# A five-stage convolution kernel on one Trainium2 core: the rows of its DRAM staging buffer take 4608 bytes instead of 4096

## The chip, the core and the metric

The kernel runs on one core of a Trainium2 chip. The metric is the device time of one execution in microseconds (us). Before the change the median of three runs is 16687.61 us.

## The reference, cut to what matters

```python
# x: (4, 512, 512, 16)
def _L0_conv_ref(x, h0, numerators, denumerator):      # the convolution by FFT
    H_full = h0 + H_cc                                 # (16, 16, 1024, 513), from two 8x8 polynomials
    X = jnp.fft.rfft2(x, s=(2 * l1, 2 * l2), axes=(-3, -2))
    Y = jnp.einsum('...hwi,ijhw->...hwj', X, H_full)   # 16x16 channel mix at each frequency
    y = jnp.fft.irfft2(Y, s=(2 * l1, 2 * l2), axes=(-3, -2))
    return y[..., :l1, :l2, :]

x = x + _L0_conv_ref(_gn(x), h0, numerators, denumerator)   # group norm, convolution, add
x = x + _L1_conv_ref(_gn(x), kernel, bias, radius)          # a 3x3 layer, not touched here
```

The change lies in the middle of the first line: the convolution of all rows of the half-transformed image with the half-transformed filter.

## The kernel before, in words

The kernel is written with the Tile framework, which puts in the semaphore waits. It has five stages, one after the other: the filter (`filter_phase`), the transform of the image along one axis (`forward_phase`), the convolution along the other axis (`conv_phase`), and the inverse transform and the 3x3 layer (both in `last_phase`). The stages hand their results over in DRAM: `g_d` holds the filter, `x_d` the image, `y_d` the result of the convolution. Rows of these buffers carry a padding of `PITCH` = 1024 elements already.

`conv_phase` takes the stretch from about 4.7 ms to 13.7 ms. It works through 513 rows `n`, one frequency of the first axis each (row 0 is done as two). For each row it transforms the image row, multiplies it with the filter at 128 frequencies `f`, and transforms back. The image row must be there in eight copies that are shifted against each other by 16 partitions (`C` = 16), so that one matmul per frequency does the work of a short convolution. The parts of one row are:

- `load_x` (L748) brings the image row into `x`, `x_part` (L777) multiplies it on TensorE with the row's own transform matrix into `px`, and the result is copied into part 0 of `xe`, a tile of 128 partitions with eight parts of 1024 fp32 (4096 bytes) each.
- `x_late` stores part 0 to the DRAM buffer `xf_d[n % 4]`, makes the rotated other half `xl` with six operations on GpSimd (L798, L799, L800), and stores that too. Both stores go out from GpSimd's queue at L791. Each writes 112 rows of 4096 bytes. `half_shift` (L809) makes part 4 of `xe` on ScalarE without DRAM.
- `load_xe` (L815) reads the other six parts back, as two DMAs of 1.5 MB from SP's queue. DMA `t` (1 and 5) gives partition p, part t + i, the row p + 16 (t + i) of `xf_d`, for i from 0 to 2. Each is therefore 384 pieces of 4096 bytes, and most rows are read several times.
- `load_g` (L736) brings the filter row, 1 MB, and `g_part` (L829) transforms it into `gh`.
- `mix` (L845) multiplies `gh` with `xe`; `over_q` (L866 to L884) and `over_g` (L903, L914) transform back and store to `y_d` from GpSimd's queue.

`step(n)` fixes the order. It starts with `load_x(n + 3)`, `load_g(n + 2)` and `load_xe(n + 1)`. Then come four quarters; each holds a quarter of `mix(n)`, of `g_part(n + 1)` and of `over_q(n - 1)`, and the first quarter also `x_part(n + 2)` and `x_late(n + 2)`. So the stores of a row are issued one step ahead of its loads, and its loads one step ahead of its `mix`. In the trace SP issues in the order first `xe` load, `g`, second `xe` load, `x`, and the first of them waits for the landing of the second store.

`XF` is the length of a row of `xf_d` in elements: 128 x 2 x 4 = 1024, which is 4096 bytes. A buffer is `[16 * C, XF]`, 256 rows without a gap.

Of the kernel before, what the change touches and what calls it, by code (L numbers as in the profile page):

```python
# [40 lines left out]
F32 = mybir.dt.float32  # L41
# [5 lines left out]
P = 128  # L47
N = 512
B = 4
C = 16  # L50
# [4 lines left out]
Y_ROW = 2 * B * S * C * 8  # L55
PITCH = 1024
XF = F * 2 * B
GN_EPS = 1e-5
L1_EPS = 1e-12

# [143 lines left out]
def bc(ap, axis, shape):  # L204
    return ap.unsqueeze(axis).to_broadcast(shape)
# [328 lines left out]
def group_stats(nc, pool, psum, mean_m, eps_t, mv):  # L534

    mu = pool.tile([P, 8], F32, name="gn_mu")
    nc.vector.tensor_copy(mu, mv[:, :, 0])
    pm = psum.tile([P, 8], F32, name="gn_ps", tag="gn_ps")
    nc.tensor.matmul(pm, mean_m, mu, start=True, stop=True)
    mean = pool.tile([P, 8], F32, name="gn_mean")  # L540
    nc.vector.tensor_copy(mean, pm)
    d = pool.tile([P, 8], F32, name="gn_d")
    nc.vector.tensor_sub(d, mu, mean)
    nc.vector.tensor_mul(d, d, d)
    nc.vector.tensor_add(d, d, mv[:, :, 1])
    pv = psum.tile([P, 8], F32, name="gn_ps2", tag="gn_ps")
    nc.tensor.matmul(pv, mean_m, d, start=True, stop=True)
    sd = pool.tile([P, 8], F32, name="gn_sd")
    nc.scalar.activation(sd, pv, AF.Sqrt, bias=eps_t)
    scale = pool.tile([P, 8], F32, name="gn_scale")  # L550
    nc.vector.reciprocal(scale, sd)
    bias = pool.tile([P, 8], F32, name="gn_bias")
    nc.vector.scalar_tensor_tensor(bias, mean, -1.0, scale, ALU.mult, ALU.mult)
    return scale, bias
# [36 lines left out]
def joined(nc, pool, a, b):  # L591

    mv = pool.tile([P, 8, 2], F32, name="mv")
    d = pool.tile([P, 8], F32, name="mv_d")
    nc.vector.tensor_add(mv, a, b)
    nc.vector.tensor_scalar(mv, mv, 0.5, None, ALU.mult)
    nc.vector.tensor_sub(d, a[:, :, 0], mv[:, :, 0])
    nc.vector.tensor_mul(d, d, d)
    nc.vector.tensor_add(mv[:, :, 1], mv[:, :, 1], d)
    return mv  # L600


def forward_phase(tc, cst, x, mvs, x_d):
    nc = tc.nc
    with ExitStack() as ctx:
# [13 lines left out]
        eps_t = cp.tile([P, 1], F32, name="x_eps")  # L619
        nc.gpsimd.memset(eps_t, GN_EPS)  # L620
        norm = [group_stats(nc, sm, ps_s, mean_m, eps_t, joined(nc, sm, mvs[2 * b], mvs[2 * b + 1]))
# [74 lines left out]
def conv_phase(tc, cst, g_d, x_d, y_d):  # L696
    nc = tc.nc
    with ExitStack() as ctx:
# [14 lines left out]
        ig = load_const(nc, cp, cst, "ig").rearrange("p (s c n) -> p s c n", s=4, c=2)  # L713
        late = load_const(nc, cp, cst, "late").rearrange("p (v f) -> p v f", v=3)

        xf_d = [tc.dram_tile([16 * C, XF], F32, name=f"xf_d{n}") for n in range(4)]


        rows = [(0, 0, 0), (0, 0, 1)] + [(n // P, n % P, None) for n in range(1, N)]
# [64 lines left out]
        def x_late(n):  # L784

            xe = state["xe", n][:, 0]
            fl = xe.rearrange("p f h c k -> p f (h c k)")

            def store(half, t):
                at = slice(C, P) if half == 0 else slice(0, P - C)  # L790
                nc.gpsimd.dma_start(out=xf_d[n % 4][half * P :, :][at], in_=t[at].rearrange("p f x -> p (f x)"))  # L791

            store(0, fl)
            xl = xlp.tile([P, F, 2, 2, 2], F32, name="xl")
            u = xlp.tile([P, F, 2, 2, 2], F32, name="xu")
            for c in range(2):
                for h in range(2):
                    nc.gpsimd.tensor_mul(u[:, :, h, c], xe[:, :, h, 1 - c], bc(late[:, 1 + c], 2, [P, F, 2]))  # L798
            nc.gpsimd.tensor_mul(xl.rearrange("p f h c k -> p f (h c k)"), fl, bc(late[:, 0], 2, [P, F, 8]))  # L799
            nc.gpsimd.tensor_add(xl.rearrange("p f h c k -> p (f h c k)"),  # L800
                                 xl.rearrange("p f h c k -> p (f h c k)"),
                                 u.rearrange("p f h c k -> p (f h c k)"))
            store(1, xl.rearrange("p f h c k -> p f (h c k)"))
            state["xl"] = xl
# [7 lines left out]
        def load_xe(n):  # L812
            src = xf_d[n % 4]
            for t in (1, 5):
                nc.sync.dma_start(  # L815
                    out=state["xe", n][:, t : t + 3].rearrange("p t f h c k -> p t (f h c k)"),
                    in_=bass.AP(tensor=src.tensor, offset=src.offset + t * C * XF,
                                ap=[[XF, P], [C * XF, 3], [1, XF]]),
                )

        def g_part(n, j):
# [100 lines left out]
        def step(n):  # L922
# [9 lines left out]
            if row(1):  # L932
                load_xe(n + 1)
# [29 lines left out]
def last_phase(tc, cst, x, y_d, yw_d, t_d, kern, bias, radius, out):  # L963
    nc = tc.nc
    with ExitStack() as ctx:
# [11 lines left out]
        eps_t = cp.tile([P, 1], F32, name="l_eps")  # L977
        nc.gpsimd.memset(eps_t, GN_EPS)
        eps1 = cp.tile([P, 1], F32, name="l_eps1")
# [409 lines left out]
def body(tc, ins, cst, out):  # L1389
    g_d = [tc.dram_tile([P, G_ROW + PITCH], F32, name=f"g_d{r}") for r in range(4)]  # L1390
    x_d = [tc.dram_tile([P, X_ROW + PITCH], F32, name=f"x_d{r}") for r in range(4)]
    y_d = [tc.dram_tile([P, Y_ROW + PITCH], F32, name=f"y_d{r}") for r in range(4)]
    yw_d = [tc.dram_tile([C, N, N], F32, name=f"yw_d{b}") for b in range(B)]
    t_d = [[tc.dram_tile([N, P, C], F32, name=f"t_d{b}_{w}") for w in range(4)] for b in range(B)]
    with tc.tile_pool(name="s_mv", bufs=2 * B) as mp:
        mvs = []
        with tc.tile_pool(name="s_in", bufs=1) as xp:
            beside = image_stats(tc, xp, mp, ins["x"], mvs)
            filter_phase(tc, cst, ins["L0_conv_h0"], ins["L0_conv_numerators"][0],
                         ins["L0_conv_denumerator"], g_d, beside)  # L1400
            for _ in beside:
                pass
        forward_phase(tc, cst, ins["x"], mvs, x_d)
    conv_phase(tc, cst, g_d, x_d, y_d)
    last_phase(tc, cst, ins["x"], y_d, yw_d, t_d, ins["L1_conv_kernel"], ins["L1_conv_bias"],
               ins["L1_conv_radius"], out)
# [30 lines left out]
```

## Time and profile before

| what | value |
|---|---|
| median of three runs | 16687.61 us (16677.77 to 16700.49) |
| the profiled execution's own time | 16676.9 us |
| its span, first to last instruction | 16675.0 us |
| granted TensorE clock, mean | 0.970 |
| TensorE busy in the span | 15084.4 us, 90% |
| DMA traffic | 4543.40 MB, mean 272 GB/s |
| `xe` loads from `xf_d` | 1026, 1536.0 KB each |
| stores into `xf_d` | 2 x 513, 448.0 KB each |

The engines are TensorE (PE for its matmuls, PEld for its weight loads), VectorE (DVE), ScalarE (ACT), GpSimd (POOL) and SyncE (SP, which only issues DMAs). The profile comes from one execution. A line such as "PE pm L845 <- DMA xe<-xf_d" says that TensorE sat idle ahead of an instruction of line 845, which writes `pm`, until that DMA had landed; "issue" stands for idle time with no cause in the profile. Beside the instructions the trace has a record of each DMA packet, with its queue, start, length of time and size; q1 is the queue of SP and q0 that of GpSimd.

### The profile page before, as it was taken

The numbers are of one execution on the slowest core, as the hardware profiler recorded it, in microseconds if no ns is written. First come the engines' busy times: TensorE is split into PE (matmuls) and PEld (weight loads), VectorE is DVE, ScalarE is ACT, GpSimd is POOL, SyncE is SP. The second block draws the span as 40 slices with busy tenths as digits, with TensorE's granted clock in tenths as the row PEclk, the third lists the DMA queues.
The fourth block names the chain that finished last, engine by engine and source line by source line (L and its number), as shares of the span: only waits on it lengthen the run. The fifth ranks groups of instructions, "written<-read, shape, count | busy, mean of one in ns | idle before, by whom it ended". The sixth has DMA issues, their size and how long they took to land. (4 is left out here: it accounts for less than half of the span.)

```text
span 16675.0 us, 545650 instructions
## 1 busy us (share of the span) xinstructions
PE 15084.4 (90%) x232588; PEld 11256.3 (68%) x232588; DVE 10610.7 (64%) x22299; ACT 9049.8 (54%) x18799; POOL 10372.0 (62%) x10669
## 2 busy tenths in 40 slices
PE   7999999998988898888888898888888888988888
PEld 5555555554557777777777777777777777867777
DVE  8999999993545555555555555555555552357877
ACT  5666666663345555555555555555555551027888
POOL 7777777772346666666666666666666660237766
PEclk7999999999999999999999999999999999989999
DMA  4888788878878888888888888888888886885531
GB/s 134 231 237 236 233 241 234 237 227 259 248 267 323 325 326 317 321 320 318 321 324 324 325 325 321 324 324 321 324 321 321 324 322 230 312 291 164 169 108 70
DMA packets 2914698, 4543.40 MB, mean 272 GB/s; under 512 B 126114, under 2 KB 2094460, under 8 KB 2801422
## 3 DMA queue, kind: packets, MB, share of 16 engines
q1 hardware_dynamic: 2703070, 3836.37, 67.4%
q0 software_dynamic: 172336, 605.00, 9.4%
q10 hardware_dynamic: 36864, 67.13, 1.2%
q8 instruction: 1833, 30.03, 0.7%
q14 instruction: 595, 4.87, 0.1%
HBM read 3030.71 MB, written 1477.31 MB: 270 GB/s over the span
## 5 line engine op out<-in xcount | busy, mean ns | idle before, releaser
L829 PE MATMUL pg<-c_dg,g 64*128 64x128 f32 x32832 | 2837.4, 290 | 357.0 <-ACT gh L729 186.6
L845 PE MATMUL pm<-xe,gh 128*32 128x64 f32 x131328 | 2386.6, 222 | 538.5 <-issue 286.2
L845 PEld LDWEIGHTS pm<-xe,gh 128*32 128x32 f32 x131328 | 2007.6, 110 | 1133.5 <-issue 933.1
L829 PEld LDWEIGHTS pg<-c_dg,g 64*128 64x128 f32 x32832 | 2286.2, 190 | 692.3 <-issue 260.3
L874 DVE TENSOR_TENSOR z<-zq,pz 128x256 f32<-128x256 f32 x2052 | 861.6, 420 | 2667.5 <-ACT zq L873 2597.6
L727 DVE COPY gh<-pg 128x512 f32<-128x512 f32 x2046 | 1409.9, 689 | 1242.8 <-PE pg L829 1237.6
L449 PE MATMUL pt<-ev_in,c_todd 128*128 128x512 f32 x4096 | 1928.0, 609 | 108.6 <-ACT u L337 83.4
L798 POOL TENSOR_TENSOR xu<-xe,c_late 128x256 f32<-128x256 f32 x2052 | 1394.3, 705 | 863.7 <-ACT xe L729 842.8
L506 DVE RECIPROCAL dn<-dn 128x256 f32<-128x256 f32 x1024 | 1718.1, 1718 | 0.0
L729 ACT COPY yf<-pm 128x512 f32<-128x512 f32 x2046 | 1211.0, 592 | 915.4 <-PE pm L845 901.4
L381 POOL TENSOR_TENSOR sp<-m,dn 128x512 f32<-128x512 f32 x1024 | 1302.6, 1273 | 611.8 <-DVE dn L506 527.1
L809 ACT COPY xe<-xl 64x1024 f32<-64x1024 f32 x513 | 538.7, 1050 | 1895.8 <-POOL xl L800 1895.8
L449 PEld LDWEIGHTS pt<-ev_in,c_todd 128*128 128x128 f32 x4096 | 728.6, 190 | 1022.1 <-issue 701.5
L729 ACT COPY gh<-pg 128x512 f32<-128x512 f32 x2058 | 1201.2, 584 | 378.9 <-PE pg L829 376.6
L866 PE MATMUL pz<-c_ident,yf 128*128 128x128 f32 x8208 | 1372.2, 290 | 29.9 <-issue 17.3
L397 PEld LDWEIGHTS pg<-c_dinv,sp 64*128 64x128 f32 x16384 | 1004.2, 196 | 466.2 <-ACT sp L386 211.4
L408 ACT COPY st<-pg 128x256 f32<-128x256 f32 x2048 | 617.6, 391 | 1281.9 <-PE pg L397 1281.9
L800 POOL TENSOR_TENSOR xl<-xl,xu 128x1024 f32<-128x1024 f32 x513 | 1209.7, 2358 | 40.2
L397 PE MATMUL pg<-c_dinv,sp 64*128 64x128 f32 x16384 | 1106.6, 287 | 72.4 <-ACT sp L386 48.3
L882 POOL TENSOR_TENSOR zd<-z 128x512 f32<-128x512 f32 x513 | 653.1, 1273 | 771.7 <-DVE z L874 771.7
L914 POOL DMA_DIRECT2D y_d<-yo x511 | 297.3, 582 | 1332.6 <-ACT yo L729 1306.8
L1280 PE MATMUL pc<-l_band,xn 128*128 128x160 f32 (+2 forms) x6144 | 1072.9, 333 | 52.2 <-DVE e_o L1335 51.9
(211 smaller groups left out, 30943.8 us busy)
## 6 DMA issues: line engine op xcount, KB each, us to landing
xe<-xf_d SPq DMA_DIRECT2D x1026, 1536.0 KB
g<-g_d SPq DMA_DIRECT2D x511, 1024.0 KB
g_d<-st SPq DMA_DIRECT2D x256, 1024.0 KB
ev_in<-g_d SPq DMA_DIRECT2D x1024, 256.0 KB
g_d<-ot SPq DMA_DIRECT2D x1024, 256.0 KB
xf_d<-xe POOLq DMA_DIRECT2D x513, 448.0 KB, 8.3
xf_d<-xl POOLq DMA_DIRECT2D x513, 448.0 KB, 5.5
x_d<-xo SPq DMA_DIRECT2D x128, 1024.0 KB
```

The costliest lines, as they stand in the source:

```text
L381: nc.gpsimd.tensor_mul(w["sp"], w["m"], bc(w["dn"], 2, [P, 2, 2, P]))
L397: nc.tensor.matmul(pg[u][:, n, k].rearrange("p a x -> p (a x)"), w["sp"][q, k, c, :], dinv[q, 2 * kp + k, c, :], start=(c == 0), stop=(c = ...
L449: nc.tensor.matmul(pt, todd[:, c, kc, hh * P : hh * P + P], ev[:, kc, c], start=(kc == 0), stop=(kc == 1),)
L506: nc.vector.reciprocal(w["dn"], w["dn"])
L727: nc.vector.tensor_copy(dst, src)
L729: nc.scalar.copy(dst, src)
L798: nc.gpsimd.tensor_mul(u[:, :, h, c], xe[:, :, h, 1 - c], bc(late[:, 1 + c], 2, [P, F, 2]))
L800: nc.gpsimd.tensor_add(xl.rearrange("p f h c k -> p (f h c k)"), xl.rearrange("p f h c k -> p (f h c k)"), u.rearrange("p f h c k -> p (f ...
L829: nc.tensor.matmul(pg[c][:, j % 4], g[half, j], dg[half], start=True, stop=True)
L845: nc.tensor.matmul(pm[32 * q : 32 * q + 32, g % 8], gh[:, f].rearrange("p c j -> p (c j)"), xe[:, :, f].rearrange("p t h c k -> p t (h c k ...
L866: nc.tensor.transpose(pz[:, t % 4].rearrange("p v q x -> p (v q x)"), y[:, at].rearrange("p g x -> p (g x)"), ident)
L1280: nc.tensor.matmul(pc[:, lo:hi, :].rearrange("p w j -> p (w j)"), xns[q][:, h * P + dh : h * P + dh + P], bands[dh][:, o : o + hi - lo, :] ...
```

## The change

A new constant `XP` = `XF` + 128 elements is the distance from row to row in the four `xf_d` buffers: 1152 elements, 4608 bytes. The rows still hold 1024 elements, and the last 512 bytes of each are neither written nor read. The stores write the first `XF` columns, and the two loads step by `XP` and `C * XP`. The amount of data moved, the number of DMAs and all work of the engines are the same in the code.

```diff
 XF = F * 2 * B
+XP = XF + 128
...
-        xf_d = [tc.dram_tile([16 * C, XF], F32, name=f"xf_d{n}") for n in range(4)]
+        xf_d = [tc.dram_tile([16 * C, XP], F32, name=f"xf_d{n}") for n in range(4)]
...
-                nc.gpsimd.dma_start(out=xf_d[n % 4][half * P :, :][at], in_=t[at].rearrange("p f x -> p (f x)"))
+                nc.gpsimd.dma_start(out=xf_d[n % 4][half * P :, :XF][at], in_=t[at].rearrange("p f x -> p (f x)"))
...
                     out=state["xe", n][:, t : t + 3].rearrange("p t f h c k -> p t (f h c k)"),
-                    in_=bass.AP(tensor=src.tensor, offset=src.offset + t * C * XF,
-                                ap=[[XF, P], [C * XF, 3], [1, XF]]),
+                    in_=bass.AP(tensor=src.tensor, offset=src.offset + t * C * XP,
+                                ap=[[XP, P], [C * XP, 3], [1, XF]]),
```

## The prediction

> **What bounds the kernel now.** I read the page first, for the stage and its costs. The edit touches only the convolution stage; the filter, forward and last stages neither write nor read `xf_d`, so the chain that ended last, which stays in the last stage, says nothing here.
>
> ```profile
> span 16675.0 us, 545650 instructions
> ...
> DMA packets 2914698, 4543.40 MB, mean 272 GB/s; under 512 B 126114, under 2 KB 2094460, under 8 KB 2801422
> ...
> xe<-xf_d SPq DMA_DIRECT2D x1026, 1536.0 KB
> g<-g_d SPq DMA_DIRECT2D x511, 1024.0 KB
> ...
> xf_d<-xe POOLq DMA_DIRECT2D x513, 448.0 KB, 8.3
> xf_d<-xl POOLq DMA_DIRECT2D x513, 448.0 KB, 5.5
> ```
>
> The `xe` loads are 3 MB of the some 5.4 MB that a row moves (1 MB is `g`, 0.25 `x`, 0.875 the two stores, 0.25 `y`). Next the table of stretches, for 8500 us in the even part of the stage.
>
> ```profile
> core 0: us, PE busy (x) PEld busy (x) DVE busy (x) ACT busy (x) POOL busy (x), PEclk, DMA share, GB/s
> 5000.00:13500.00 8500.00, 7599.34 (x173522) 6083.54 (x173522) 4630.72 (x12533) 4488.84 (x8195) 5435.32 (x5303) 0.98 0.87 322
> ```
>
> TensorE is busy 7599 of 8500 us (89%) and the 16 DMA engines 87%. Two resources are nearly full; the others are at half to two thirds. Who makes the other wait is in the waits of TensorE and of SP's queue in nearly the same stretch.
>
> ```profile
> PE pm L845 <- issue: 256.9, 279, 3.2
> PE pg L829 <- ACT gh L729: 177.0, 195, 3.9
> PE pg L829 <- issue: 153.1, 92, 3.4
> PE pm L845 <- DMA xe<-xf_d: 110.7, 75, 3.5
> ```
>
> ```profile
> SPq L815 <- DMA xf_d<-xl: 5849.9, 453, 15.1
> SPq L748 <- PE px L777: 1021.6, 441, 6.6
> ```
>
> The fourth line is the one that the change can reach directly: 110.7 us of TensorE's time in 8500 us goes to `xe` loads that land late. The SP lines show that the loads start as soon as the second store has landed: that landing is itself a link of the loop.
>
> The waits put down few rows to the DMA, so I measured it from the records: in 485 rows of the stage, the end of the last `xe` packet against the first matmul of that row's first `mix` quarter. The shortest distance is some 0.6 us and a heap of rows lies at 0.7 to 0.85: the landing signal. In 148 of the 485 (31%) the matmul starts under 0.9 us after the last packet, with a TensorE gap of 1.06 us in the mean ahead of it. Those rows are set by the DMA; in the others TensorE comes to the row later (median distance of all rows 1.7 us). The row takes 17.65 us in the mean.
>
> **What the skill says.** The Trainium skill, "DMA: Bandwidth & Descriptors", section "Latency and other measured facts", warns of HBM row pitches at large powers of two: copies at a pitch of 512 KiB ran at 207 GB/s, at 4 MiB at 103, and a padding of 4 KiB brought the full rate back while 192 B didn't. Nothing there covers a pitch of 4 KiB, and its cause is given as an inference. The trace shows a far milder case: 86% of the `xe` packets take 150 to 159 ns, which is a floor (159 ns is also their median, and 4096 B in 159 ns on 16 engines is 412 GB/s). The same page, "How a descriptor splits into AXI transactions", counts transactions of 256 B from an aligned start: 4608 is 18 x 256, so a row stays 16 transactions. The same page's "Why a DMA increments its semaphore by 16 and not by 1" takes the number of engines from the slowest dimensions, 128 and 112 before and after, so 16 engines remain. No run here shows the last two apart.
>
> **The change, part by part.**
>
> *What stays at nothing.* Each store and load has the same rows, bytes and pieces (384 packets a load, as counted in the records: 768 a row), so GpSimd's issue (0.57 to 0.58 us each) and SP's (0.37 to 0.43) keep their price. No wait is added or moved: both loads already wait for both stores. The arithmetic isn't touched. TensorE's "issue" idle, the largest, follows the 16 KB packets of a queue of its own (1002 ns in the mean, TensorE going on 1.2 to 1.5 us after them), whose source is not `xf_d`; I leave it as it is.
>
> *The loads.* In the stretch the `xe` packets take 175.3 ns in the mean against the floor of 159: 16.3 ns x 768 / 16 engines = 0.78 us of the row's DMA time. In the first load it is 179.3, and its first 24 packets take 311, the next 197 and 192: all engines start together there, 4 partitions (16 KB of DRAM) apart, and reach the floor after about 1.5 us. That start costs (152 + 38 + 33) x 24 / 16 = 0.33 us. The second load, with 171.6, is slow in its first half. A collision of engines that start at addresses with the same low bits would look like this, and 4608 would put 4 rows 18 KB apart. For it speaks also that in the same stage the `g` packets, 8192 B from a pitch of 8192 (32 KB for 4 partitions), take 369 against a floor of 309, 19% over, while the `x` packets of 2048 B take 84.6 against 84. Against it speaks that any cold start may look so.
> Bounds: all of it gained is -0.78 us; as slow as `g` is 159 x 1.19 = 190 ns, +0.69 us. I take half the excess away, 167 ns: **-0.4 us** a row.
>
> *The stores.* Their packets (with those of `y`) take 168.1 ns; 224 x 9.1 / 16 = 0.13 us at most to gain. I take nothing.
>
> *From DMA time to row time.* With the gaps of the 148 rows, a landing that is earlier by d gives back the smaller of d and the gap: d = 0.4 gives 0.112 us a row over all 485, d = 0.8 gives 0.189. A later landing costs what exceeds the distance: 0.052 us a row at 0.2, 0.122 at 0.4, 0.204 at 0.6, 0.293 at 0.8. What is late next in the rows that gain is TensorE itself, with its own "issue" idle and the wait for ScalarE's `gh`. The rows that gain nothing hide the loads behind TensorE's 15.7 us of work a row. I count no gain from the store's landing a little earlier.
>
> *Sum.* 513 rows x 0.112 = **57 us**. Against the profiled execution 16676.9 (span 16675.0 and 1.9 around it) that is 16620; its time lies 0.06% under the median of the runs, so against 16687.6 it is **16630 us, -0.34%**.
>
> **The rivals.**
>
> *No effect (chance 0.26).* The excess is the cold start of a burst and reads that stand behind other reads, and neither sees the pitch. For it: 86% at the floor already, and the slowness of `g` changes from row to row (309 to 483) with no period of a power of two that I could find. Then 16688, within 0.2% (33 us).
>
> *Slower, by unsettled starts (0.16).* With 4096 every packet starts at the same place of a 4 KB block, and once the engines have sorted themselves they stay apart: that is the floor after 1.5 us. With 4608 each row starts 512 B further on, seven of eight packets lie across a block's edge, and the order could break again and again. Price: up to the ratio of `g`, 190 ns, +0.69 us a row, 0.245 us a row by the table between 0.6 and 0.8, x 513 = 126 us: 16813. It decides when the mean packet is above some 180.5 ns (+5.2 x 48 = 0.25 us, 0.07 x 513 = 36 us).
>
> *The rows don't stay one packet (0.04).* If a piece across an edge is cut in two, the pieces cost like the 2048 B packets of `x`, 84 each: 168 for 159 on seven eighths, 7.9 x 48 = 0.38 us, 0.115 x 513 = 59 us: 16747. The number of packets would show it.
>
> **How the numbers follow.** The forecast case, a packet mean under about 170.5 ns, has 0.54. It reaches from the 0.2% mark to the whole excess (0.187 x 513 = 96 us: 16592), and a little beyond, where a shorter queue also brings the stores home earlier: 16570. The two slower cases together have 0.20; I take in their nearer half, to 16765. Below 16570 I leave 0.07 and above 16765 0.11. Under 0.2% (33 us) of change is about what a measurement of this kernel can't tell from none. Range of the likeliest case alone: 16570 to 16655. Faster 0.54, same 0.26, slower 0.20.
>
> **What would show it.** The packets of `xe` from q1: mean under 170 ns, and the first 24 of a row well under 311. "PE pm L845 <- DMA xe<-xf_d" falls from 110.7 us to some 70, and the DMA share from 0.87 towards 0.85, with the same bytes. The row falls from 17.65 to 17.54 us. Filter, forward and last stages keep their lengths. I am wrong if the packets don't get shorter (no effect), if they pass 180 (slower), or if they get shorter and the row doesn't, which would mean that TensorE's own idle takes the place of the wait.

## The result, and the profile after

The kernel after takes 16595.06 us in the median of four runs (16587.33 to 16608.49), against 16682.69 us for the kernel before on the same chip. The ratio is 0.9948, with a 95% interval of 0.9931 to 0.9965: 0.52% less, some 87 us, where 57 us were forecast. A later repeat beside other kernels gave 0.9954 (0.9941 to 0.9968). The two programs have the same instructions on each engine. Only the addresses differ.

The profiled execution took 16601.06 us. These are the page's lines for the kernel after:

```profile
span 16599.1 us, 545650 instructions
...
DMA packets 2914698, 4543.40 MB, mean 274 GB/s; under 512 B 126114, under 2 KB 2094460, under 8 KB 2801422
...
xf_d<-xe POOLq DMA_DIRECT2D x513, 448.0 KB, 8.2
xf_d<-xl POOLq DMA_DIRECT2D x513, 448.0 KB, 5.5
```

The packets, their sizes and their bytes are what they were, so no row was cut in two, and the stores land after 8.2 and 5.5 us, where it was 8.3 and 5.5. The even part of the convolution stage, in the table of stretches of the kernel after (columns as in the line for before):

```profile
5000.00:13500.00 8500.00, 7635.76 (x174840) 6117.06 (x174836) 4654.47 (x12628) 4518.41 (x8256) 5473.24 (x5342) 0.99 0.87 325
```

TensorE did 174840 matmul instructions in these 8500 us instead of 173522, 0.8% more. From the first `mix` matmul to the last the stage is 8963.3 us long instead of 9040.3. These 77 us are the whole difference of the spans, 75.9. The waits of TensorE in that stretch, kernel after (us in total, times, longest):

```profile
PE pm L846 <- issue: 220.3, 247, 3.2
PE pg L830 <- ACT gh L730: 206.3, 228, 3.8
PE pg L830 <- issue: 140.0, 93, 2.9
PE pm L846 <- DMA xe<-xf_d: 81.0, 72, 3.0
```

The wait for `xe` fell by 30 us. The two "issue" waits fell by 50 us, from 256.9 and 153.1, and the wait for ScalarE's `gh` grew by 29. The DMA share stayed at 0.87, since more rows go through in the same time (325 GB/s instead of 322). The prediction had left the "issue" idle out of its sum.

### The profile page after: what moved, and what is told of

Read it like the earlier page. It is cut to its first block, busy times and chain, and to the rows that moved or that the text cites. A ratio compares the mean times of both kernels' runs of the same rounds, so it can differ in the third digit from the quotient of the medians.

```text
span 16599.1 us, 545650 instructions
## 1 busy us (share of the span) xinstructions
PE 15057.2 (91%) x232588; PEld 11240.5 (68%) x232588; DVE 10596.9 (64%) x22299; ACT 9042.9 (54%) x18799; POOL 10362.7 (62%) x10669
## 3 DMA queue, kind: packets, MB, share of 16 engines
q8 instruction: 1833, 30.03, 0.7%
```

## The experiments

Twelve runs were made. The first seven ask what part of the change brings the gain, the eighth what TensorE waits for, the ninth how little padding serves, and the rest repeats and looks for a better kernel. Where a diff is against the kernel after, it says so. "The end of the loads" is the mean time from the issue of a row's first `xe` load to the end of its last `xe` packet, taken from the packet records over 482 rows.

**The spread of the kernel before.** No edit.

> The kernel before, unchanged, as a measure of the spread. All theories: ratio 1.000 within 0.002. Its records tell how far the packet means move from one execution to the next: xe packets 175 ns, g packets 369 ns, idle of TensorE for xe loads 111 us in 8500. If g packets come out near 347 ns here too, their shortening after the change was chance.

Measured: ratio 1.000 (0.9992 to 1.0009). But its waits moved a good deal from one execution to the next:

```profile
PE pm L845 <- issue: 330.6, 336, 3.2
PE pg L829 <- issue: 150.5, 93, 3.3
PE pg L829 <- ACT gh L729: 136.5, 163, 3.8
PE pm L845 <- DMA xe<-xf_d: 84.3, 67, 2.9
```

The wait for `xe` is 84.3 us here with no change at all, so its fall to 81.0 proves nothing. Nor does a single line of the others: the first "issue" line went from 256.9 to 330.6 us and the wait for `gh` from 177.0 to 136.5, each more than it moved with the change. The `g` packets take 363 ns, not 347.

**The place of the buffers alone.**

```diff
-        xf_d = [tc.dram_tile([16 * C, XF], F32, name=f"xf_d{n}") for n in range(4)]
+        xf_d = [tc.dram_tile([18 * C, XF], F32, name=f"xf_d{n}") for n in range(4)]
```

> Pitch stays at 4096 bytes, each buffer gets 32 rows that nobody uses, so that it is as long as with the pitch of 4608. Theory A, the pitch (addresses of rows): ratio 1.000 within 0.002, g packets about 369 ns. Theory B, the place of the buffers in DRAM (they start 1.125 MB apart instead of 1 MB): ratio about 0.995, g packets about 347 ns, as after the change.

Measured: 1.0015 (1.0008 to 1.0021), end of the loads 15.20 us. The place gives no gain, rather a loss of 0.15%; theory B falls. The `g` packets take 354.5 ns here, at the old pitch, against 369 and 363 in the two executions of the kernel before: their length is no measure of the pitch.

**A pitch of 8192 bytes.** Against the kernel after:

```diff
-XP = XF + 128
+XP = XF + 1024
```

> Pitch of 8192 bytes: still a power of two, and every row begins at a multiple of 4096. Theory A, in the form that equal low address bits of the rows collide: no gain, ratio 1.000 or above, g packets 369 ns or more. Theory B, the place of the buffers: some change in either sense, since they lie 2 MB apart. If any pitch but 4096 helps (rows no longer back to back): 0.995.

Measured: 1.0196 (1.0181 to 1.0212), the largest effect of all, and on the wrong side for "any pitch but 4096". The stretch and the waits of this kernel:

```profile
5000.00:13500.00 8500.00, 7454.22 (x167464) 5962.84 (x167466) 4495.20 (x12091) 4359.59 (x7908) 5233.07 (x5115) 0.96 0.86 311
```

```profile
PE pm L846 <- issue: 424.2, 331, 3.5
PE pg L830 <- issue: 191.0, 101, 3.9
PE pm L846 <- DMA xe<-xf_d: 157.1, 85, 5.2
```

The first load's packets take 221 ns in the mean, against 179 in the kernel before and 184 in the kernel after, and the end of the loads is 0.87 us later than in the kernel before (16.05). Nothing but the distance of the rows, and with it the length and place of the buffers, is different from the kernel after. The "issue" waits grow with the DMA time, too.

**A pitch of 5120 bytes** (`XP = XF + 256`).

> Pitch of 5120 bytes (1024 more, not 512). Theory A, rows spread over the low address bits: gain as with 4608, ratio 0.993 to 0.997, g packets about 347 ns. Theory B, the place: no reason for the same gain, as the buffers lie 1.25 MB apart.

Measured: 0.996 (0.9947 to 0.9973), end of the loads 15.01 us.

**A pitch of 8192 + 512 bytes** (`XP = XF + 1152`).

> Pitch of 8192 + 512 bytes. Theory A, the rows' low address bits (rows of engines that start together[...] must not lie a multiple of a large power of two apart): the loss of the 8192 pitch is gone and the gain of the 4608 pitch is there, ratio 0.993 to 0.997, first load's packets back from 221 to some 184 ns. Theory C, distance alone (rows that are further apart cost more): stays slow, ratio 1.015 or above, first load's packets 215 ns or more.

Measured: 0.9949 (0.9936 to 0.9963), first load's packets 185 ns, end of the loads 15.03 us. 512 bytes more turn the worst kernel into one as fast as the kernel after. So it is not the distance that costs; theory C falls. Of the pitches tried, the two that are multiples of 4096 bytes are the slow ones.

**Stores at 4608, loads at 4096, and the other way round.** Both start from the kernel after and fill the buffers with zeros once. Loads and stores then no longer mean the same rows, so the values differ; the traffic stays. In the first the loads step by the old pitch:

```diff
-                    in_=bass.AP(tensor=src.tensor, offset=src.offset + t * C * XP,
-                                ap=[[XP, P], [C * XP, 3], [1, XF]]),
+                    in_=bass.AP(tensor=src.tensor, offset=src.offset + t * C * XF,
+                                ap=[[XF, P], [C * XF, 3], [1, XF]]),
```

> The buffers are long enough for 4608, the stores step by 4608 bytes and the loads by 4096, so that the loads bring other bytes of the same stores and the convolution's values are different; buffers are filled with zeros once before the stage, some 10 us. Waits and traffic stay. If the gain comes from the reads: as with the placement alone (buffers 32 rows longer), ratio 1.000 to 1.003, the end of the loads 15.2 us after their issue. If it comes from the writes: ratio 0.995 to 0.998, end of loads 15.0 us.

In the second the stores do:

```diff
-                nc.gpsimd.dma_start(out=xf_d[n % 4][half * P :, :XF][at], in_=t[at].rearrange("p f x -> p (f x)"))
+                first = C if half == 0 else P
+                rows = xf_d[n % 4].rearrange("a b -> (a b)")[first * XF : (first + P - C) * XF]
+                nc.gpsimd.dma_start(out=rows.rearrange("(a b) -> a b", b=XF), in_=t[at].rearrange("p f x -> p (f x)"))
```

> The other half: stores step by 4096 bytes and loads by 4608, other bytes of the same stores, the convolution's values differ, and the zeros once before the stage. If the gain comes from the reads: ratio 0.995 to 0.998, end of loads 15.0 us after their issue. If it comes from the writes: 1.000 to 1.003, and 15.2 us.

Measured: 1.0008 (1.0 to 1.0016) with the stores alone changed, 0.995 (0.9936 to 0.9963) with the loads alone. The end of the loads is at 15.25 and 14.96 us. The zeros put the first `mix` matmul off by 16 us (4803 instead of 4787), 0.1% that both ratios contain. The gain is that of the reads; the writes bring nothing.

**Half of the filter loads left out**, in the kernel before:

```diff
+            if n >= 5 and n % 2:
+                state["g", n] = g_of[0]
+                return
             rc, r, plane = rows[n]
             g = io.tile([P, C, 8 * C], F32, name="g")
+            g_of[0] = g
```

> The kernel before at a pitch of 4096, in which every second row takes over the filter row of the row ahead of it instead of loading its own, so the result of these rows is another one; half of the g loads fall away, 128 packets x 369 ns / 16 = 2.95 us in every second row, 1.5 us a row in the mean. If the gaps of single rows bound what an earlier landing gives back, as the prediction's table had it, no more than 0.32 us x 513 = 165 us, ratio 0.990 or above. If a row that comes earlier makes the next stores and loads earlier too, so that a row follows the end of its loads by some seven tenths until TensorE alone sets it: 0.7 us or more a row, ratio 0.980 or below.

Measured: 1.0034 (1.002 to 1.0048), slower than before. That lies within the bound of the first theory (0.990 or above) and far from the second, but neither of them has room for a loss. The waits of TensorE:

```profile
PE pm L850 <- issue: 512.5, 433, 4.6
PE pg L834 <- issue: 139.9, 90, 4.0
PE pg L834 <- ACT gh L730: 110.4, 138, 3.8
PE pm L850 <- ACT zq L878: 101.9, 274, 0.6
```

The loads end 11.8 us after their issue instead of 15.2, and the wait for `xe` is gone from the list; yet the row isn't shorter. The wait with no cause has grown from 256.9 to 512.5 us and eaten all of it. Taking the wait for `xe` away did not shorten the row. This sent me to the "issue" idle.

**A pitch of 4352 bytes** (`XP = XF + 64`).

> Pitch of 4352 bytes, 256 more. If any pitch off the power of two serves: ratio 0.993 to 0.997 as with 512 and 1024 more, end of loads 15.0 us after issue. If what counts is a shift of 512 or more from row to row[...]: half the gain or none, 0.997 to 1.001, 15.1 to 15.2 us.

Measured: 0.9964 (0.9951 to 0.9976), end of the loads 15.03 us. 256 bytes are enough.

**The kernel after once more, and with the filter's rows spread too.** The second differs from the kernel after in `g_d`, at every place that steps through it; this is the core:

```diff
-G_ROW = 2 * S * C * 8 * C
+GP = C * 8 * C + 128
+G_ROW = 2 * S * GP
...
-                nc.sync.dma_start(out=t, in_=dram(g_d[rc], r, 0, [w, P], [1, w]))
+                nc.sync.dma_start(out=t, in_=dram(g_d[rc], r, 0, [GP, P], [1, w]))
```

It was run twice, the second time beside the kernel after.

> The kernel after, and beside it the rows of the filter in g_d take 8704 bytes instead of 8192 (512 bytes more for each of 128 partitions). Theory A: the g packets, 346 ns after the change against 309 for the shortest, fall to 325 or less, that is 0.17 us or more of DMA time a row; with a row following the loads' end by some seven tenths, some 60 us more, ratio to before about 0.991. If g's packets are slow only because they stand behind those of xe: they stay above 340 ns, ratio as after the change, 0.995.

> The kernel after once more, beside the next one. Ratio 0.995 within 0.0015, xe packets 177, g packets 347 ns, end of loads 15.0 us.

> The kernel after with the rows of the filter in g_d at 8704 bytes, once more beside the kernel after. In the first run its convolution stage was as long as that of the kernel after and its filter stage 10 us shorter. If that holds, it is 10 us (0.06%) ahead of the kernel after; if it was chance, level with it.

Measured: 0.9934 (0.9922 to 0.9946) the first time; the second time 0.9948 (0.9934 to 0.9961) beside 0.9954 (0.9941 to 0.9968) for the kernel after. In the first run the `g` packets take 346.5 ns as in the kernel after, and in the second 354 beside 351: 512 bytes more between their rows change nothing, so this reading of mine, that their own rows slow them, falls. The convolution stage is not shorter (8971.3 and 8955.6 us, against 8963.3 and 8948.4). The filter stage, which writes and reads `g_d` too, issues its last store at 3899.4 and 3897.7 us instead of 3908.8 and 3909.0. These 9 to 11 us are seen in both profiles, and both ratios are the lowest among the kernels run beside them, but the intervals overlap, and with no change to `g_d` the same store already moves between 3904.8 us (the pitch of 4352) and 3909.2.

## Why: what TensorE waits for

The chain of thought starts from a stretch of the kernel before. This is its timeline, TensorE's matmuls only (start, length, line, count, idle ahead of it):

```profile
9012.90 0.98 PE L845 MATMUL pm<-xe,gh 128*32 128x64 f32 x54
9015.05 0.38 PE L845 MATMUL pm<-xe,gh 128*32 128x64 f32 x10 [1.17 <-issue]
9015.36 1.16 PE L829 MATMUL pg<-c_dg,g 64*128 64x128 f32 x16
```

A block of 64 matmuls that need the same data stops after 54 for more than a microsecond. No data can be missing there. The page of the kernel before shows a queue that moves nothing of the kernel's own tensors:

```profile
q8 instruction: 1833, 30.03, 0.7%
```

30.03 MB in 1833 packets are 16384 bytes each. In the stretch of 200 us from 9000 on there are 32 of them and 8228 instructions of TensorE, 257 a packet; in the whole 8500 us it is 255.8. That makes 64 bytes an instruction, 256 in a packet. So I numbered TensorE's instructions in the stage. Gaps of over 250 ns that end 1.0 to 1.7 us after the end of a q8 packet fall on one position of 256: in the kernel before 466 gaps are at number 193, and no other position has more than 11. It is the same 193 in all fourteen profiles of this study. TensorE runs dry at the seam of two packets of its program.

The Trainium skill, "Runtime: NRT & Kernel Launch", section "Instruction fetch mechanics", says that an engine's sequencer fetches its instructions in blocks of 16 KiB (256 instructions) by a DMA of its own while it runs the block before, and that the crossing is "mostly hidden". The size agrees. The hiding doesn't in this stage: of 1363 seams in 8500 us of the kernel before, 465 cost 1.27 us each, 589 us in all. This counts the stop of the weight loads, which begins ahead of that of the matmuls (1.33 us against 1.17 at the gap above); the matmuls alone are idle at these seams for some 480 us.

The packets of q8 start later while the row's loads are in flight. In the kernel before, a block's packet starts 1.29 us after TensorE has crossed the seam ahead, if that falls 16 to 18 us after the row's loads were issued, when they are done; it starts 3.89 us after it, if that falls at 6 to 8 us, in the middle of the loads. The seams whose packet starts late are those with a gap: 0.85 us in the mean at 6 to 8 us, 0.04 at 16 to 18. A row holds 2.8 seams in the mean, at other places each time. That the packets stand behind those of the loads on the same DMA engines is the reading I hold; the records do not name a packet's engine, and the memory could delay them as well.

The table has the means of the runs, from the records. "Packets" is the time of all packets of a row on one of 16 engines, "seams" TensorE's gaps at the seams, "wait for xe" the profile's line over 8500 us.

| kernel | packets, us a row | end of loads, us | start of q8 packet after the seam, us | seams, us a row | wait for xe, us | row, us |
|---|---|---|---|---|---|---|
| before | 15.33 | 15.18 | 2.99 | 1.22 | 110.7 | 17.65 |
| before again | 15.32 | 15.16 | 3.07 | 1.43 | 84.3 | 17.67 |
| 4096, longer buffers | 15.36 | 15.20 | 3.07 | 1.37 | 98.1 | 17.67 |
| stores 4608, loads 4096 | 15.34 | 15.25 | 3.07 | 1.37 | 127.3 | 17.75 |
| after (4608) | 15.22 | 14.96 | 2.91 | 1.09 | 81.0 | 17.50 |
| after again | 15.19 | 14.96 | 2.92 | 1.12 | 88.1 | 17.48 |
| stores 4096, loads 4608 | 15.20 | 14.96 | 2.84 | 0.99 | 111.2 | 17.45 |
| 4352 | 15.14 | 15.03 | 2.86 | 1.02 | 106.0 | 17.54 |
| 5120 | 15.25 | 15.01 | 2.90 | 1.06 | 93.6 | 17.51 |
| 8704 | 15.30 | 15.03 | 3.01 | 1.28 | 74.7 | 17.56 |
| 8192 | 15.69 | 16.05 | 3.24 | 1.68 | 157.1 | 18.28 |

The loads at 4096 stand together in packets, end of loads and row; so do those at the padded pitches. The mean of the first four rows is 1.35 us at the seams, that of the next six 1.09: 0.26 us less, which is more than the 0.18 us that the row is shorter (17.69 to 17.51); other waits grow in their place (`gh` from 136.5 to 177 us before, 199 and 206 in the two profiles of the kernel after). The wait for `xe` overlaps between the two groups.

Not all of the 0.18 us is idle time. In the same two groups the matmuls' idle falls from 1.89 to 1.79 us a row, and their busy time from 15.79 to 15.71, with the same work. The tables of stretches show the reason: the granted clock PEclk is 0.98 before, 0.99 after and 0.96 at 8192. In the trace the clock falls to half for 3.4 us at a time (now and then 6.8): 76 times in 8500 us of the kernel before, 62 times in the kernel after, 157 times at 8192. It does so after long stops. Of the 68 stops of the matmuls of over 2 us in the kernel before, 53 had a half clock begin in them or within 3.5 us of their end; of the 723 stops of 0.25 to 1.3 us none had. A long stop, at a seam or elsewhere, is thus paid for twice.

That the loads' pitch sets the end of the loads and the length of the row is shown, by undoing it each way. That the row follows by way of the seams, rather than by the wait for `xe`, is argued and not shown. For it speak the places of the gaps, and the kernel with half of the filter loads, whose wait for `xe` is gone while its seams cost 1.77 us a row and the row is no shorter. Against it speaks that the seams, too, move by themselves: from 1.22 to 1.43 us between two executions of the kernel before, whose rows are equal (17.65 and 17.67), and with the pitch of 8704 they cost 1.28 in a row of 17.56. No kernel changed the fetches alone; that was not tried.

## The prediction, point by point

- **The bound.** Right in its two full resources, wrong in the link. The wait for `xe` that "the change can reach directly" is the smaller part of TensorE's idle, and moves between 84 and 111 us by itself.
- **"I leave it as it is"**, of the "issue" idle. This is the step that failed. The prediction saw that this idle follows 16 KB packets of a queue of their own, and took it that their source not being `xf_d` kept them clear of the change. They were not clear of it: in the means of the two groups their start moved from 3.05 to 2.91 us after the seam, and the idle at the seams from 1.35 to 1.09 us a row, where the prediction had nothing. How much of the row's gain this carries stays open, as said above; the faster clock after fewer long stops, 0.08 us a row, was not in the sum either.
- **The loads.** The sign of the DMA time was right, its size and its place were not. Forecast was a mean packet of 167 ns for `xe` and 311 ns well undercut for the first 24; measured were 176.7 and 405 (340 in the repeat). In this pair of profiles the packets that got shorter are those of `g`, from 369 to 347 ns, and the row's packets together lost 0.11 us, not 0.4. By the end of the loads it is 0.22 us. The length of one stream's packets says little: those of `g` took 355 ns with the loads at 4096 and the longer buffers and 356 at 4352, and at 8192, where the first load's packets took 221 ns, those of `g` fell to 320.
- **From DMA time to row time.** The table gave back 0.112 for 0.4 us, a share of 0.28. Measured is 0.15 us of row (17.65 to 17.50) for 0.22 us of loads, 0.7, and with the pitch of 8192 0.63 for 0.87, again 0.7. The term was too small by a factor of 2.5, and it stood on the gaps of the wrong wait. The two errors, too much gained in the loads and too little passed on, went against each other, and 57 us came out for 87. That it came so near is luck.
- **"What would show it."** None of the signs from the DMAs came: the `xe` packets did not get shorter (175.3 ns before, 176.7 after), the DMA share stayed at 0.87, and the wait for `xe` moved no more than between two executions of the kernel before. The prediction took packets that don't get shorter as the sign of "no effect"; yet the row fell to 17.50 us, further than the 17.54 forecast. The end of the loads is what shows the change.
- **The stores at nothing.** Right: 1.0008 with the stores alone. The time from the issue of the second store to that of the next loads is 5.52 us in the mean before and after, so the landing gave nothing either.
- **The rivals.** "No effect" and a cut of the rows in two are excluded by the ratio and by the count of packets. A net loss by unsettled starts is excluded too: 256, 512 and 1024 bytes more all gain.
- **"Filter, forward and last stages keep their lengths"**: right. The first `mix` matmul starts at 4786.2 us before and 4786.9 after.

What stays open: why reads at a pitch of 4096 or 8192 bytes are slower, by which wait the row follows the loads, and why leaving half of the filter loads out makes the seams dearer. In that kernel the two `xe` loads follow each other without `g` between them, and 218 of its seams instead of 155 fall at 6 to 8 us after the issue of the loads, where a packet starts 4.24 us after the seam. That this is the reason is argued from one profile, not shown.

## What to carry to other kernels

Try another distance between the rows of a DRAM buffer that is read back by many partitions when it is 4096 or 8192 bytes: here 256 to 1024 bytes of padding gained 0.36 to 0.52%, and doubling the pitch, which looks like padding as well, lost 2%. Where an engine idles in the middle of a block whose data is there, count its instructions modulo 256: its own program comes by DMA, and here its packets started later while large loads were in flight. Price a DMA saving against that idle too, and not only against the waits that name the transfer, and look at the granted clock after long stops. Before reading a single wait as the cause, see how far it moves between two executions of the same kernel.

## What the runs showed of the hardware

- Rows of 4096 bytes read by 128 partitions: the loads of a row end 15.2 us after their issue at a pitch of 4096 bytes, 15.0 us at 4352, 4608, 5120 and 8704, and 16.05 us at 8192, with the same packets and bytes. The first load takes 179 to 184 ns a packet at 4096, 178 to 185 at the padded pitches, and 221 at 8192.
- TensorE's instructions come in packets of 16384 bytes of 256 instructions; a packet took 1.0 us, started 1.3 us after the seam before it when the row's loads were done and 3.9 us after it in their midst, and TensorE went on 1.2 to 1.6 us after its end. In the kernel before a third of the seams cost 1.3 us.
- After stops of over 2 us TensorE's granted clock fell to half for 3.4 us or more in 53 of 68 cases, after stops of under 1.3 us in none of 723 (kernel before).
- A fifth less of the loads' time (11.8 instead of 15.2 us), by leaving out half of the filter loads, made the row no shorter.
